# Message rows in three staggered steps, and a norm's chain moved among the projections

## The chip, the cores and the metric

The kernel runs on one core of a Trainium2 chip. The metric is the device time of one execution in microseconds (us), as the median of several runs. Every profile line below comes from one profiled execution.

The core has five engines with a queue each, and each works through its own queue in order: TensorE (PE in the profile, its weight loads PEld), VectorE (DVE), ScalarE (ACT), GpSimd (POOL) and SyncE (SP). DMAs are issued from the engines' queues, most of them here from SyncE's.

## What is computed

Four layers run one after another on an image batch of 4 x 128 x 128 x 128, each on the group-normalized output of the one before, with the result added to it: a deformable convolution, a scan of 1-d convolutions over rows, a message layer and a triangle layer. The change touches the last two. Cut to what matters:

```python
def _L2_conv_ref(inputs, Wself, Wm, Wk):
    message_m = jnp.sum(inputs, axis=2)
    message_k = jnp.sum(inputs, axis=1)
    z_self = jnp.einsum('bmkd,hd->bmkh', inputs, Wself)
    z_m = jnp.einsum('bmd,hd->bmh', message_m, Wm)[:, :, None, :]
    z_k = jnp.einsum('bkd,hd->bkh', message_k, Wk)[:, None, :, :]
    return z_self + z_m + z_k
...
    xn = layer_norm(x, norm_g, norm_b)
    left = xn @ left_w + left_b
    right = xn @ right_w + right_b
    left = left * jax.nn.sigmoid(xn @ lgate_w + lgate_b)
    right = right * jax.nn.sigmoid(xn @ rgate_w + rgate_b)
    out_gate = jax.nn.sigmoid(xn @ ogate_w + ogate_b)
    out = jnp.einsum('bkjd,bkid->bijd', left, right)
    out = layer_norm(out, onorm_g, onorm_b) * out_gate
    return out @ to_out_w + to_out_b
...
    x = x + _L2_conv_ref(_gn(x), L2_conv_Wself, L2_conv_Wm, L2_conv_Wk)
    x = x + _L3_conv_ref(_gn(x), L3_conv_norm_g, L3_conv_norm_b, L3_conv_left_w, L3_conv_left_b, L3_conv_right_w, L3_conv_right_b, L3_conv_lgate_w, L3_conv_lgate_b, L3_conv_rgate_w, L3_conv_rgate_b, L3_conv_ogate_w, L3_conv_ogate_b, L3_conv_onorm_g, L3_conv_onorm_b, L3_conv_to_out_w, L3_conv_to_out_b)
```

`_gn` normalizes groups of four channels over a whole image. So each layer needs the sums of all rows of an image before it can scale the first.

## The kernel before, in words

The first layer runs from the start to about 3340 us, the scan layer to about 4120 us, and the last two layers, in `message_and_triangle`, from there to the end at 5763 us. That function holds one whole image in SBUF (X, 128 channels by 128 by 128), the triangle's left factors and later its output (L), and two buffers R for a quarter of the channels of the right factors. R also takes quarters of the scan's output x2 from HBM, for the message rows of the next image.

For each image the work runs in these stages. All are lists of small Python functions, and `weave` deals pieces of several lists out in proportion to their lengths. The order of each engine's queue is the order in which the pieces are called: the scheduler is set to manual for all five engines (`manual_schedule`). A piece puts instructions into several queues at once, and those queues then run on their own.

1. **The norm of x2 (`prelude`, L1273).** A chain of small operations that goes to and fro between TensorE, VectorE and ScalarE: the group mean (L130 and L132), the variance (L134 to L140), square root and reciprocal (L86 to L90), the scaled weights ws, the sums msg and their products (L1277 to L1288), and the message vectors z with the channel sums (L1290 to L1302). It is one piece of the list.
2. **Message rows (`sums_of`, rows at L1315).** 32 blocks of four rows (JB = 4). A block is a product of ws with four rows of R into PSUM on TensorE (self_ps, L1319), four sums with the messages into X on VectorE (L1325), and one square with an accumulated sum on ScalarE (junk, L1330). All three stand in one piece. PSUM holds two such blocks (pool ps_q). After the block that empties a buffer R the next quarter of x2 is fetched into it. The pieces means, variances and close then give the scale for X.
3. **Turning (`turned`, L1401).** Four groups of 32 columns. A block of four columns is scaled (ScalarE, L1409), transposed on TensorE (turn_ps, L1419), copied back into X by ScalarE (L1420), and counted by bn_stats on VectorE (L1422). At the end of a group `factors` gives mean and reciprocal deviation.
4. **Spreading and projecting (`spread`, `projected`).** VectorE normalizes the turned columns (normed, L1439), TensorE transposes them back (back_ps, L1448), ScalarE copies (L1449). TensorE makes the gate and the left and right projections (proj_ps, L1479), eight columns to a piece, ScalarE their sigmoid (work, L1483), and VectorE two gated products into L and R (L1485). The first two quarters of the channels are projected among turning and spreading.
5. **Later projections and triangles (`projected`, `triangle`).** The third and fourth quarter, sixteen pieces each, are woven with eight pieces of the triangle product of the quarter before (tri_ps, L1497, copied to L by ScalarE, L1501). Then the last quarter's triangle runs alone.
6. **Output (`counted_out`, `given`).** VectorE counts columns of L (stats_o, L1512). A step of `given` loads a gate and x3 from HBM, normalizes four columns (two on VectorE, L1545, two on ScalarE, L1540), transposes them (gT_ps, L1555), scales them on ScalarE (work, L1557), multiplies by the gate on GpSimd (L1558), and in the step after that makes the output product (out_ps, L1565 and L1569), copied to res by ScalarE in odd steps (L1572) and by VectorE in even ones (L1574), and stored.

The next image's stages 1 and 2 and its first group of turning, together the list `ahead`, are woven into the output of the image before: the first six pieces (FIRST = 6) with the first group of counting, the others with the output steps. Image 0's run alone before, and nothing follows image 3's output. The columns of the last triangle are the first that the counting reads, so counting can't begin before the last copy into L.

Of the kernel before, what the change touches and what calls it, by code (L numbers as in the profile page):

```python
# [9 lines left out]
F32 = mybir.dt.float32  # L10
I32 = mybir.dt.int32
BF16 = mybir.dt.bfloat16
AF = mybir.ActivationFunctionType
# [5 lines left out]
P = 128  # L19
# [1155 lines left out]
def message_and_triangle(tc, c, x2T, x3d, gates, counted, w2, w3, out):  # L1175
# [15 lines left out]
    with ExitStack() as ctx:  # L1191
# [76 lines left out]
        def small_ps(shape, name):  # L1268
            return ps_g.tile(shape, F32, name=name, tag="ps_g")
# [2 lines left out]

        def prelude(b):  # L1273

            _, _, s2, t2 = gn_part(nc, c, two, two, ps_g, counted2[:, b], "x2", "ps_g")
            ws = one.tile([P, P], F32, name="ws")
            nc.vector.scalar_tensor_tensor(ws, wself, s2, c.ident, ALU.mult, ALU.add)  # L1277
            tsum = two.tile([P, 1], F32, name="tsum")
            nc.vector.tensor_scalar(tsum, t2, float(S), None, ALU.mult)
            msg = one.tile([P, 2, S], F32, name="msg")  # L1280
            nc.vector.tensor_scalar(msg[:, 0], sum_w[:, b], s2, tsum, ALU.mult, ALU.add)
            nc.vector.tensor_scalar(msg[:, 1], sum_h[:, b], s2, tsum, ALU.mult, ALU.add)
            twide = one.tile([P, S], F32, name="twide", tag="junk")
            nc.vector.tensor_scalar(twide, c.ones, t2, None, ALU.mult)
            pm = small_ps([P, 2, S], "msg_ps")
            nc.tensor.matmul(pm[:, 0], lhsT=wm, rhs=msg[:, 0], start=True, stop=False)
            nc.tensor.matmul(pm[:, 0], lhsT=wself, rhs=twide, start=False, stop=True)
            nc.tensor.matmul(pm[:, 1], lhsT=wk, rhs=msg[:, 1], start=True, stop=True)  # L1288
            z = one.tile([P, 2, S], F32, name="z")
            nc.vector.tensor_copy(z, pm)  # L1290
            zs = one.tile([P, 1], F32, name="zs")
            nc.vector.tensor_reduce(zs, z.rearrange("p a s -> p (a s)"), AX.X, ALU.add)
            sx = one.tile([P, 1], F32, name="sx")
            nc.vector.tensor_reduce(sx, sum_w[:, b], AX.X, ALU.add)
            pw = small_ps([P, 1], "sum_ps")
            nc.tensor.matmul(pw, lhsT=ws, rhs=sx, start=True, stop=True)
            less = two.tile([P, 1], F32, name="less3")
            nc.vector.scalar_tensor_tensor(less, zs, float(S), pw, ALU.mult, ALU.add)
            nc.vector.tensor_scalar(less, less, -1.0 / (S * S), None, ALU.mult)
            nc.vector.tensor_scalar(z[:, 1], z[:, 1], outb, None, ALU.add)  # L1300
            lessb = two.tile([P, 1], F32, name="lessb3")
            nc.vector.tensor_tensor(lessb, less, outb, ALU.subtract)  # L1302
            squares = two.tile([P, S // JB], F32, name="squares")
            got[b] = (ws, z, less, lessb, squares)

        def fetch(b, i):

# [2 lines left out]

        def sums_of(b):

            todo = [lambda: prelude(b)]

            def rows(y0):  # L1315
                ws, z, less, lessb, squares = got[b]
                at = y0 % DQ
                pz = ps_q.tile([P, JB, S], F32, name="self_ps", tag="ps_q")
                nc.tensor.matmul(  # L1319
                    pz, lhsT=ws, rhs=R[y0 // DQ % 2][:, at : at + JB, :], start=True, stop=True  # L1320
                )
                if at + JB == DQ and y0 + DQ < S:
                    fetch(b, y0 // DQ + 2)
                for i in range(JB):
                    nc.vector.scalar_tensor_tensor(  # L1325
                        X[:, :, y0 + i], pz[:, i], z[:, 0, y0 + i : y0 + i + 1], z[:, 1],
                        ALU.add, ALU.add,
                    )
                junk = one.tile([P, S, JB], F32, name="junk", tag="junk")
                nc.scalar.activation(  # L1330
                    junk, X[:, :, y0 : y0 + JB], AF.Square, bias=lessb,
                    accum_out=squares[:, y0 // JB : y0 // JB + 1],
                )

            todo += [lambda y0=y0: rows(y0) for y0 in range(0, S, JB)]
# [65 lines left out]
        def turned(b, g):  # L1401

            stats = two.tile([P, JG, 6], F32, name="stats_x")
            todo = []

            def scale(k):
                s3, t3 = got[b]
                js = slice(g * JG + k * JB, g * JG + (k + 1) * JB)
                nc.scalar.activation(X[:, js, :], X[:, js, :], AF.Identity, bias=t3, scale=s3)  # L1409

            def block(k):
                j0 = g * JG + k * JB
# [106 lines left out]
        def given(b):  # L1519
# [41 lines left out]
            def put(k):  # L1561
                xr, a = pend[k]
                po = ps_g.tile([P, JB, P], F32, name="out_ps", tag="ps_g")
                for j in range(JB):
                    nc.tensor.matmul(  # L1565
                        po[:, j], lhsT=xr[:, j], rhs=c.ident, is_transpose=True,
                        start=True, stop=False,
                    )
                    nc.tensor.matmul(po[:, j], lhsT=a[:, j], rhs=outw, start=False, stop=True)  # L1569
                res = three.tile([P, JB, P], F32, name="res")  # L1570
                if k % 2:
                    nc.scalar.copy(res, po)  # L1572
                else:
                    nc.vector.tensor_copy(res, po)  # L1574
                pend[k] = res
# [26 lines left out]
        def run(todo):  # L1602
            for f in todo:
                f()
# [99 lines left out]
```

## Time and profile before

| what | value |
|---|---|
| runs shown | 5764.49, 5773.65, 5774.59 us; median 5773.65 |
| the profiled execution | 5764.99 us, its span 5763.2 us |
| granted TensorE clock, mean | 0.956 |
| busy over the span | PE 5261.4 (91%), PEld 4488.0 (78%), DVE 3294.4 (57%), ACT 2781.5 (48%), POOL 779.5 (14%) |
| message rows of image 0, alone | 4138 to 4182 us |
| start of the projections, images 0 to 3 | 4220.9, 4629.3, 5035.7, 5442.0 us |
| message rows of images 1 to 3 (first to last sums) | 4439.0 to 4552.0, 4847.0 to 4958.2, 5253.3 to 5364.4 us |
| bn_stats of the turning waiting for ScalarE's copy (L1422) | 92.8 us in 88 waits |

How to read it: the busy time of an engine over the span is a mean of stages that differ, so the stages are looked at one by one. A line of waits reads "engine tile line <- who ended the wait: us in total, times, longest". In a list in order of time, a line is the start, the length, engine, line, operation, output <- input and shape, and in square brackets how long the engine had been idle and for whom.

### The profile page before, as it was taken

What the parts mean: (1) busy time and instruction counts of PE and PEld (TensorE: products, weight loads), DVE (VectorE), ACT (ScalarE), POOL (GpSimd) and SP (SyncE); (2) the same over time, 40 slices, a digit from 0 to 9 for tenths busy, and PEclk for the clock granted to TensorE, in tenths of its full rate; (3) what the DMA queues carried; (4) which work ended last, traced back from release to release, by engine and by line L of the source; (5) the groups of instructions that cost most, each with busy time, mean ns of one, the idle gap of its engine ahead of it and who ended that gap; (6) DMA issues with size and microseconds to landing.
All of it is one profiled execution on the core that took longest, in us unless ns stands there. A gap on an engine that the chain in (4) does not pass through costs nothing. (4 is left out here: it accounts for less than half of the span.)

```text
span 5763.2 us, 112068 instructions
## 1 busy us (share of the span) xinstructions
PE 5261.4 (91%) x42401; PEld 4488.0 (78%) x42401; DVE 3294.4 (57%) x10355; ACT 2781.5 (48%) x5852; POOL 779.5 (14%) x674
## 2 busy tenths in 40 slices
PE   2899999999999999999999979999788798798797
PEld 1778888888888888888888879999567577576686
DVE  5544444554444644444333279999865665656656
ACT  1355554455554555545544423333264664654755
POOL 2022111002110011111000012222100200201102
PEclk9899999999999999999999989999899899898899
DMA  4555555555554555555434222223221622513515
GB/s 145 135 138 131 136 129 120 127 124 136 128 134 107 129 129 134 131 125 124 93 75 80 54 86 89 89 90 98 96 115 58 209 88 94 199 59 128 192 41 167
DMA packets 1132346, 671.45 MB, mean 117 GB/s; under 512 B 736461, under 2 KB 1002894, under 8 KB 1113366
## 3 DMA queue, kind: packets, MB, share of 16 engines
q1 hardware_dynamic: 1121650, 657.77, 43.1%
q8 instruction: 338, 5.54, 0.4%
q10 hardware_dynamic: 10148, 6.43, 0.4%
q14 instruction: 210, 1.72, 0.1%
HBM read 382.88 MB, written 281.11 MB: 115 GB/s over the span
## 5 line engine op out<-in xcount | busy, mean ns | idle before, releaser
L509 DVE TENSOR_TENSOR m<-ty,t_ps 120x390 f32<-120x390 f32 x1548 | 804.5, 556 | 1503.6 <-ACT ty L507 1502.4
L520 PEld LDWEIGHTS v_ps<-m,pixels 120*128 120x128 f32 x11352 | 1439.2, 194 | 86.4 <-issue 10.1
L520 PE MATMUL v_ps<-m,pixels 120*128 120x108 f32 (+1 forms) x11352 | 1465.4, 273 | 3.6 <-ACT v L530 3.5
L530 ACT COPY v<-v_ps 128x432 f32<-128x432 f32 x1376 | 718.9, 522 | 1273.9 <-PE v_ps L520 1271.1
L578 PE MATMUL conv_ps<-v,wdef 128*128 128x128 f32 (+2 forms) x5160 | 1304.0, 379 | 5.0 <-DVE x1c L551 4.5
L578 PEld LDWEIGHTS conv_ps<-v,wdef 128*128 128x128 f32 x5160 | 814.2, 193 | 255.7 <-issue 24.9
L507 ACT COPY ty<-t_ps 120x390 f32<-120x390 f32 x1560 | 688.1, 489 | 179.4 <-PE t_ps L497 172.0
L497 PE MATMUL t_ps<-places,spread 25*120 25x99 bf16 (+1 forms) x10836 | 521.2, 260 | 63.2 <-DVE m L509 39.7
L497 PEld LDWEIGHTS <-spread 25*120 25x120 bf16 x10896 | 339.9, 137 | 225.4 <-issue 124.8
L1479 PEld LDWEIGHTS proj_ps<-wcat,X 128*128 128x128 f32 x4096 | 473.1, 192 | 29.6 <-issue 28.6
L1479 PE MATMUL proj_ps<-wcat,X 128*128 128x128 f32 x4096 | 480.6, 275 | 1.4
L392 POOL TENSOR_TENSOR off<-off,koff 72x512 f32<-72x512 f32 x128 | 162.1, 1267 | 2298.3 <-DVE off L389 2205.3
L1068 ACT ACTIVATE rowT<-x1T_ps,t_x,s_x 128x128 f32<-128x128 f32 x512 | 192.7, 457 | 366.4 <-PE x1T_ps L1061 346.8
L1558 POOL TENSOR_TENSOR work<-work,gate 128x512 f32<-128x512 f32 x128 | 163.3, 1276 | 1495.5 <-ACT work L1557 1245.4
L1081 PE MATMUL m_ps<-carry,w 128*128 128x172 f32 x2286 | 361.3, 310 | 0.0
L1485 DVE TENSOR_TENSOR L<-proj_ps,work 128x256 f32<-128x256 f32 x256 | 154.6, 604 | 340.5 <-ACT work L1483 340.5
L1081 PEld LDWEIGHTS m_ps<-carry,w 128*128 128x128 f32 x2286 | 345.5, 188 | 0.0
L1148 POOL TENSOR_TENSOR sum_h<-sum_h,x2c 128x512 f32<-128x512 f32 x128 | 162.3, 1268 | 1163.3 <-DVE x2c L1145 1163.3
L1483 ACT ACTIVATE work<-proj_ps 128x512 f32<-128x512 f32 x256 | 151.4, 597 | 283.9 <-PE proj_ps L1479 283.9
L1569 PE MATMUL out_ps<-outw,work 128*128 128x128 f32 x1024 | 219.0, 316 | 69.6 <-POOL work L1558 69.6
L1569 PEld LDWEIGHTS out_ps<-outw,work 128*128 128x128 f32 x1024 | 182.5, 223 | 86.8 <-POOL work L1558 86.8
L1325 DVE SCALAR_TENSOR_TENSOR X<-self_ps,z 128x128 f32<-128x128 f32 x512 | 152.4, 420 | 76.5 <-PE self_ps L1319 76.2
(230 smaller groups left out, 6675.5 us busy)
## 6 DMA issues: line engine op xcount, KB each, us to landing
pixels<-tab SPq DMA_DIRECT2D x688, 123.8 KB
xin<-in_x_dram SPq DMA_DIRECT2D x56, 1024.0 KB
off<-parts SPq DMA_DIRECT2D x64, 891.0 KB
tab<-rows SPq DMA_DIRECT2D x384, 128.0 KB
places<-off SPq DMA_DIRECT2D x688, 55.7 KB
x<-x1c SPq DMA_DIRECT2D x32, 1024.0 KB
x1rows<-x SPq DMA_DIRECT2D x128, 256.0 KB
x2T<-x2c SPq DMA_DIRECT2D x128, 256.0 KB
```

Source lines behind the costliest of these rows:

```text
L497: nc.tensor.matmul(to, lhsT=spread[p0 : p0 + KROWS, ph, :], rhs=mov, start=True, stop=True,)
L507: nc.scalar.copy(ty[:, 0:n], tp[0:LANES, 0, 0:n])
L509: nc.vector.tensor_tensor(m, ty[:, 0:n].rearrange("p (r c) -> p r c", c=PADW), tx, ALU.mult)
L520: nc.tensor.matmul(vp[:, h * n : h * n + rows * w].rearrange("p (k c) -> p k c", c=w), lhsT=pix[0:LANES, xb, :], rhs=m[:, :, RX * xb : RX ...
L530: nc.scalar.copy(v[:, :, c0 : c0 + 4 * RX].rearrange("p k (h c) -> p k h c", c=RX), vp[:, 0 : 4 * n].rearrange("p (h k c) -> p k h c", h=4 ...
L578: nc.tensor.matmul(pc[:, at : at + r1 - r0, :], lhsT=wdef[:, 3 * ky + kx, :], rhs=v[:, k0 + kx, r0:r1, kx : kx + S], start=m == 0, stop=m ...
L1068: nc.scalar.activation(rt[:, b, :], px[:, b, :], AF.Identity, bias=t, scale=s)
L1081: nc.tensor.matmul(to, lhsT=wgt, rhs=src[:, :, at : at + n], start=i == 0, stop=i + 1 == len(todo),)
L1148: nc.gpsimd.tensor_tensor(sum_h, sum_h, x2c[:, :, i], add)
L1479: nc.tensor.matmul(pp[:, j], lhsT=X[:, j0 + j, :], rhs=wcat[:, cols], start=True, stop=True)
L1558: nc.gpsimd.tensor_tensor(a, a, gt, ALU.mult)
L1569: nc.tensor.matmul(po[:, j], lhsT=a[:, j], rhs=outw, start=False, stop=True)
```

## The change

- **Rows in three steps.** `rows(k)` now issues the sums of block k-1, the product of block k and the squares of block k-2. There are 34 such pieces instead of 32.
- **The chain for the norm of x2 in six pieces.** `prelude` returns mean, variance, factors_of_x2, sums, messages and close. For images 1 to 3 they are woven into the projections of the last quarter of the image before; for image 0 they stand ahead of its rows, as before.
- **Counting of turned columns one block later.** bn_stats of block k-1 is issued after the copy of block k, and the last block's in the close.
- **Result copies.** VectorE copies every fourth result instead of every second.

With the six pieces of the chain, the sixteen of the projections and the eight of the triangle, `weave` gives this order (p projection, t triangle):

```
p0 t0 mean p1 p2 t1 p3 variance p4 t2 p5 p6 factors_of_x2 t3 p7 p8 t4 sums
p9 p10 t5 p11 messages p12 t6 p13 p14 close t7 p15
```

The diff, with the bodies of the chain's pieces left out where they are the old lines:

```diff
         def prelude(b):
 
-            _, _, s2, t2 = gn_part(nc, c, two, two, ps_g, counted2[:, b], "x2", "ps_g")
-            ws = one.tile([P, P], F32, name="ws")
...
+            v = {}
+
+            def mean():
+                v["ps"] = small_ps([P, 1], "gn_ps3")
+                nc.tensor.matmul(
+                    v["ps"], lhsT=c.gmean, rhs=counted2[:, b, 0:1], start=True, stop=True
+                )
+
+            def variance():
+                v["mean"] = two.tile([P, 1], F32, name="m_x2")
+                nc.vector.tensor_copy(v["mean"], v["ps"])
...
+                nc.tensor.matmul(v["ps"], lhsT=c.gmean, rhs=d, start=True, stop=True)
+
+            def factors_of_x2():
+                var = two.tile([P, 1], F32, name="gp_var")
+                nc.vector.tensor_copy(var, v["ps"])
+                _, v["s"], v["t"] = scale_shift(nc, c, two, v["mean"], var, "x2")
+
+            def sums():
+                s2, t2 = v["s"], v["t"]
...
+                nc.tensor.matmul(pm[:, 1], lhsT=wk, rhs=msg[:, 1], start=True, stop=True)
+
+            def messages():
+                z = v["z"] = one.tile([P, 2, S], F32, name="z")
+                nc.vector.tensor_copy(z, v["ps"])
...
+                nc.tensor.matmul(v["ps"], lhsT=v["ws"], rhs=sx, start=True, stop=True)
+
+            def close():
...
+                got[b] = (v["ws"], z, less, lessb, squares)
+
+            return [mean, variance, factors_of_x2, sums, messages, close]
 
         def sums_of(b):
 
-            todo = [lambda: prelude(b)]
...
+            def rows(k):
+                if 1 <= k <= n:
+                    put(k - 1)
+                if k < n:
+                    product(k)
+                if k >= 2:
+                    square(k - 2)
+
+            todo = [lambda k=k: rows(k) for k in range(n + 2)]
...
                 nc.scalar.copy(X[:, j0 : j0 + JB, :], pt)
-                for j in range(JB):
-                    nc.vector.bn_stats(stats[:, k * JB + j, :], X[:, j0 + j, :])
+                if k:
+                    count(k - 1)
+
+            def count(k):
+                for j in range(k * JB, (k + 1) * JB):
+                    nc.vector.bn_stats(stats[:, j, :], X[:, g * JG + j, :])
 
             def close():
+                count(JG // JB - 1)
                 known["x", b, g] = factors(stats, "x")
...
-                if k % 2:
+                if k % 4:
                     nc.scalar.copy(res, po)
                 else:
                     nc.vector.tensor_copy(res, po)
...
-        run(sums_of(0) + turned(0, 0))
+        run(prelude(0) + sums_of(0) + turned(0, 0))
...
             for q in range(2, NQ):
-                run(weave(projected(b, q, 0, S), triangle(b, q - 1)))
+                run(weave(
+                    projected(b, q, 0, S), triangle(b, q - 1),
+                    prelude(b + 1) if q + 1 == NQ and b + 1 < B else [],
+                ))
```

`product`, `put` and `square` hold the old lines of a row block's product with the fetch of R, its four sums and its square.

More of the change, by code (lines that the diff above doesn't have):

```diff
@@ L1273, in prelude @@
         def prelude(b):
-            _, _, s2, t2 = gn_part(nc, c, two, two, ps_g, counted2[:, b], "x2", "ps_g")
-            ws = one.tile([P, P], F32, name="ws")
[L1277 to L1304, printed above, removed]
+            v = {}
@@ new lines, in mean @@
+            def mean():
[6 more added lines that the diff above has]
+                nc.vector.tensor_copy(v["mean"], v["ps"])
+                d = two.tile([P, 1], F32, name="gp_d")
+                nc.vector.tensor_tensor(d, counted2[:, b, 0:1], v["mean"], ALU.subtract)
+                nc.vector.tensor_tensor(d, d, d, ALU.mult)
+                nc.vector.tensor_tensor(d, d, counted2[:, b, 1:2], ALU.add)
+                v["ps"] = small_ps([P, 1], "gn_ps4")
+                nc.tensor.matmul(v["ps"], lhsT=c.gmean, rhs=d, start=True, stop=True)
@@ new lines, in factors_of_x2 @@
+            def factors_of_x2():
[4 more added lines that the diff above has]
+                s2, t2 = v["s"], v["t"]
+                v["ws"] = one.tile([P, P], F32, name="ws")
+                nc.vector.scalar_tensor_tensor(v["ws"], wself, s2, c.ident, ALU.mult, ALU.add)
+                tsum = two.tile([P, 1], F32, name="tsum")
+                nc.vector.tensor_scalar(tsum, t2, float(S), None, ALU.mult)
+                msg = one.tile([P, 2, S], F32, name="msg")
+                nc.vector.tensor_scalar(msg[:, 0], sum_w[:, b], s2, tsum, ALU.mult, ALU.add)
+                nc.vector.tensor_scalar(msg[:, 1], sum_h[:, b], s2, tsum, ALU.mult, ALU.add)
+                twide = one.tile([P, S], F32, name="twide", tag="junk")
+                nc.vector.tensor_scalar(twide, c.ones, t2, None, ALU.mult)
+                pm = v["ps"] = small_ps([P, 2, S], "msg_ps")
+                nc.tensor.matmul(pm[:, 0], lhsT=wm, rhs=msg[:, 0], start=True, stop=False)
+                nc.tensor.matmul(pm[:, 0], lhsT=wself, rhs=twide, start=False, stop=True)
+                nc.tensor.matmul(pm[:, 1], lhsT=wk, rhs=msg[:, 1], start=True, stop=True)
@@ new lines, in messages @@
+            def messages():
+                z = v["z"] = one.tile([P, 2, S], F32, name="z")
+                nc.vector.tensor_copy(z, v["ps"])
+                v["zs"] = one.tile([P, 1], F32, name="zs")
+                nc.vector.tensor_reduce(v["zs"], z.rearrange("p a s -> p (a s)"), AX.X, ALU.add)
+                sx = one.tile([P, 1], F32, name="sx")
+                nc.vector.tensor_reduce(sx, sum_w[:, b], AX.X, ALU.add)
+                v["ps"] = small_ps([P, 1], "sum_ps")
+                nc.tensor.matmul(v["ps"], lhsT=v["ws"], rhs=sx, start=True, stop=True)
@@ new lines, in close @@
+            def close():
+                z = v["z"]
+                less = two.tile([P, 1], F32, name="less3")
+                nc.vector.scalar_tensor_tensor(
+                    less, v["zs"], float(S), v["ps"], ALU.mult, ALU.add
+                )
+                nc.vector.tensor_scalar(less, less, -1.0 / (S * S), None, ALU.mult)
+                nc.vector.tensor_scalar(z[:, 1], z[:, 1], outb, None, ALU.add)
+                lessb = two.tile([P, 1], F32, name="lessb3")
+                nc.vector.tensor_tensor(lessb, less, outb, ALU.subtract)
+                squares = two.tile([P, S // JB], F32, name="squares")
+                got[b] = (v["ws"], z, less, lessb, squares)
@@ L1311, in sums_of, with product @@
         def sums_of(b):
-            todo = [lambda: prelude(b)]
-            def rows(y0):
-                ws, z, less, lessb, squares = got[b]
+            n = S // JB
+            pending = {}
+            def product(k):
+                y0 = k * JB
+                ws = got[b][0]
+                pz = ps_q.tile([P, JB, S], F32, name="self_ps", tag="ps_q")
                 at = y0 % DQ
-                pz = ps_q.tile([P, JB, S], F32, name="self_ps", tag="ps_q")
                 nc.tensor.matmul(
@@ L1323, in rows, with put, square @@
                     fetch(b, y0 // DQ + 2)
+                pending[k] = pz
+            def put(k):
+                z, pz = got[b][1], pending.pop(k)
                 for i in range(JB):
+                    y = k * JB + i
                     nc.vector.scalar_tensor_tensor(
-                        X[:, :, y0 + i], pz[:, i], z[:, 0, y0 + i : y0 + i + 1], z[:, 1],
-                        ALU.add, ALU.add,
-                    )
-                junk = one.tile([P, S, JB], F32, name="junk", tag="junk")
+                        X[:, :, y], pz[:, i], z[:, 0, y : y + 1], z[:, 1], ALU.add, ALU.add,
+                    )
+            def square(k):
+                lessb, squares = got[b][3:]
+                junk = one.tile([P, S, JB], F32, name="junk")
                 nc.scalar.activation(
-                    junk, X[:, :, y0 : y0 + JB], AF.Square, bias=lessb,
-                    accum_out=squares[:, y0 // JB : y0 // JB + 1],
-                )
-            todo += [lambda y0=y0: rows(y0) for y0 in range(0, S, JB)]
+                    junk, X[:, :, k * JB : (k + 1) * JB], AF.Square, bias=lessb,
+                    accum_out=squares[:, k : k + 1],
+                )
+            def rows(k):
[6 more added lines that the diff above has]
+            todo = [lambda k=k: rows(k) for k in range(n + 2)]
             part = {}
```

## The prediction, made before the result was known

> **What bounds the kernel now.** I read the clock first (one core, 0.956), then the page's chain of work that ended last. That chain lies wholly in the last stage, so it says nothing of the others. So I cut the third part of the program (4138 to 5763 us) into stages by the starts of its tiles and asked for busy times in each (per row: stretch, length, busy us of each engine with its instructions, TensorE's granted clock, DMA share, GB/s):
>
> ```profile
> core 0: us, PE busy (x) PEld busy (x) DVE busy (x) ACT busy (x) POOL busy (x), PEclk, DMA share, GB/s
> 4340.00:4421.00 81.00, 79.60 (x707) 79.02 (x706) 34.57 (x67) 33.75 (x57) 0.00 (x0) 1.00 0.03 11
> 4437.00:4455.00 18.00, 12.12 (x15) 3.15 (x14) 17.27 (x69) 4.28 (x11) 0.00 (x0) 0.65 0.11 40
> 4455.00:4554.00 99.00, 73.74 (x346) 49.89 (x347) 74.38 (x249) 58.54 (x122) 22.86 (x18) 0.84 0.54 185
> 4629.00:4748.00 119.00, 107.26 (x721) 85.76 (x721) 72.59 (x241) 73.22 (x122) 0.00 (x0) 0.97 0.20 76
> ```
>
> The later projections with triangles (4340 to 4421) are bound by TensorE: busy 79.6 of 81, at full clock. The message rows among the output steps (4455 to 4554, image 1's rows in image 0's output) leave every engine idle for a quarter of the time or more. What VectorE and ScalarE wait for in that window:
>
> ```profile
> ACT junk L1330 <- DVE X L1325: 37.7, 23, 2.9
> DVE X L1325 <- PE self_ps L1319: 22.9, 10, 3.9
> ```
>
> VectorE's 74.4 busy and 22.9 waiting make 97.3 of 99: it is the engine of this stage, and the wait to remove is the one for a row block's product. Where it comes from shows in the order of time at one block:
>
> ```profile
> 4543.76 1.76 PE L1319 MATMUL self_ps<-R,ws 128*128 128x512 f32 x2
> 4545.56 1.23 DVE L1325 SCALAR_TENSOR_TENSOR X<-self_ps,z 128x128 f32<-128x128 f32 x4 [3.90 <-PE self_ps L1319]
> 4546.89 0.72 ACT L1330 ACTIVATE junk<-X,lessb 128x512 f32<-128x512 f32 x1 [2.30 <-DVE X L1325]
> ```
>
> The product stands on TensorE behind an output step (which itself waits for GpSimd: 13.1 us at L1569 here). VectorE's sums stand at the head of its queue until it lands, and ScalarE's squares until the sums land: three queues in one line. In the first stage of spreading and projecting (4629 to 4748) TensorE has 107.3 of 119 and its largest wait is
>
> ```profile
> PE back_ps L1448 <- DVE normed L1439: 7.3, 9, 2.5
> ```
>
> **The rows in three steps.** Sums of block k-1 now stand one list place behind their product, and squares one behind the sums. No instruction is added, the two PSUM buffers stay, the fetch of R stays glued to its product. Between product and sums there is now an output step's time or a block of statistics, so the 22.9 us should go. What is late next is VectorE itself: 74.4 busy, less 4.5 of 9 result copies in these 18 steps (k % 4 instead of k % 2) at 0.69 us = 3.1, leaves 71.3. ScalarE gets 58.5 + 4.5 x 0.58 + one square more (0.9) = 62; TensorE's 73.7 is at clock 0.84, at full clock some 55 to 62. The stage 4437 to 4455, without such waits, runs VectorE 17.27 of 18 (96%), which would give 74; ScalarE is close behind and the copy every fourth step still waits for TensorE in line (0.8 us once now), so I take 78.5: minus 20.5 an image, three images, **-61.5**. Ends: -26 (all waits and copies gone) and -10 (ScalarE and TensorE bring half of it back). Image 0's rows (4138 to 4182) run alone; VectorE has 36.3 of 44 and waits about 0.24 in every 2.49 us for the buffer's round trip, which is unchanged: 0. R's refill has eight blocks (about 22 us) against 7.4 from issue (4131.25) to first use (4138.65): hidden; without that cover, a wait of the difference.
>
> **The norm's chain taken from between the stages.** The last triangle ends on ScalarE at 4429.6; VectorE then does one block of statistics (1.1), and the next starts at 4437.60, after the chain. That is 6.9 us, three times: **-20.7**. Nothing else is late: R's first half is issued at 4417.87 and lands by about 4425.3 (7.4 later). Image 0's chain keeps its place: 0.
>
> **The same chain among the last projections.** The built order shows TensorE's matmuls of the chain directly behind the 4th, 9th and 12th of sixteen projection blocks (the middle one after a triangle block). TensorE is the bound there, and it waits for VectorE, where the chain stands behind that block's two products, which wait for ScalarE's sigmoid. The price of such a pass is in the trace, at the end of the stage:
>
> ```profile
> 4418.79 0.83 PE L1479 MATMUL proj_ps<-wcat,X 128*128 128x128 f32 x6
> ...
> 4419.71 0.60 ACT L1483 ACTIVATE work<-proj_ps 128x512 f32<-128x512 f32 x1 [1.25 <-PE proj_ps L1479]
> 4420.34 0.58 DVE L1485 TENSOR_TENSOR L<-proj_ps,work 128x256 f32<-128x256 f32 x1 [1.62 <-ACT work L1483]
> 4420.78 0.58 DVE L1485 TENSOR_TENSOR R<-proj_ps,work 128x256 f32<-128x256 f32 x1
> ...
> 4421.41 0.38 PE L1497 MATMUL tri_ps<-L,R 128*128 128x128 f32 x1 [1.79 <-DVE R L1485]
> ```
>
> So 1.75 us to R, then the chain's own VectorE time from its rows now. Variance: a copy and three columns, 4430.73 to 4431.45 = 0.75; wait 2.5, matmul 0.38: 2.9. Sums: ws, tsum, msg up to the matmul (4432.77 to 4433.62) 0.85, and the sigmoid ahead is late, because the factors switch ScalarE to the square root and back, and the first projection after it loses about 1.4 us. Counted from the end of the block before the switch: TensorE does a triangle block (to 0.9), two projections (2.7, 4.5) and a triangle (5.4); ScalarE has the root at 2.2, a copy at 2.8, the load at 4.1, its sigmoids at 4.7 and 5.3; VectorE the two blocks' products at 5.85 and 6.95, then 0.85: 7.8. The wait is 7.8 - 5.4 = 2.4; three matmuls and twide add 1.1: 3.5. Messages: z, zs and sx, 4435.33 to 4436.45 = 1.1; wait 2.85, matmul 0.38: 3.2. Mean: 0.28. Sum 9.9 an image, **+29.7**. Who pays behind the waiting matmul: every projection and triangle after it. VectorE's own 4 to 5 us of the chain lie in its idle 46 of 81; the chain issues no DMA, so SyncE's and GpSimd's queues are not touched. Ends: +2.2 an image (matmuls only, if the waits fell into slack) and +15.
>
> Two rules of the Trainium skill speak against this placing. "ScalarE: Activation LUTs", What ACT_TABLE_LOAD costs, prices a switch of function set at a load of 1283 ns and a drain of some 1380, 2.66 us. The row here is a load of 1.28 at 4629.64, with the activation starting at 4630.94 directly behind it. By the row the delay is the 1.4 above; by the page the middle wait grows by 1.4, +4.2 in all. I keep the row. "TensorE: Matmul & The Clock Gate", What's actually happening, has TensorE fall to half clock after an idle window of about 3.4 us. In the trace the 1.79 us gap above left the clock at 1.00 (4419 to 4424), while the 6.55 us one before 4138.65 was followed by products at half pace. My gaps of 2.5 to 2.9 are nearer the first: no loss; by the page's window a gap that joined a second one could lose about 3.4/2 = 1.7 each, which is in the +15.
>
> **Statistics one block later in the turning.** VectorE's bn_stats waited for ScalarE's copy (92.8 us over the run, L1422) with the norm that TensorE waits for behind it. Moved behind the next block's copy, it finds its data ready. The close does the last block, as before. Of the 7.3 (7.7 in image 0) I count 5 in each of four images, since ScalarE's copy into the same two buffers (TensorE waits 2.1 for it) comes next: **-20**. Ends: 0 and -8.
>
> **The rest.** In the last image VectorE is the fullest engine (88.7 of 113, ScalarE 67.3); eight copies less are 5.5 us of VectorE, 4.7 more of ScalarE, of which **-3** may show; the 46 us parts with turning (ScalarE 33) I put at 0. Ends: +6 and -6.
>
> Sum: -61.5 - 20.7 + 29.7 - 20 - 3 = **-75.5**. The profiled execution took 5764.99 (span 5763.2), so 5689.5 by its own time. It lies at the lower end of the runs (5764.49, 5773.65, 5774.59); a median after could lie by either, so I add half of the 8.7 between: **5694**.
>
> **Rivals.** (1) ScalarE and TensorE take over in the rows: half of the gain turns into new waits of the copies for out_ps; 99 becomes 88. -33 instead of -61.5: 5722. For it: three engines between 62 and 74 of 99. Against: the last image runs with the same three-way coupling and VectorE there goes from operation to operation. (2) The chain costs its matmuls alone, because TensorE catches up after each wait in slack that the busy time hides: +6.6 instead of +29.7: 5671. Against it: TensorE's 79.6 of 81. (3) Slower: the chain's waits on TensorE cost the upper 15 an image, and the rows only rename their wait, because the output step's own loop through GpSimd (13.1 us of TensorE's waits) sets their pace. Then -20.7 + 45 - 5 - 3 = +16: 5786. This side begins where rows and statistics together save less than the 9 us by which the chain costs more than it frees (29.7 - 20.7). Against it: GpSimd is busy 22.9 of 99.
>
> **How the numbers follow.** Mine 0.58 (5670 to 5718), rival 1 0.20, rival 2 0.13, rival 3 0.05, and 0.04 for no visible change, where the gain is eaten by the chain. The range for 8 in 10 takes mine, rival 2 and most of rival 1: 5648 to 5740. About 0.2% (11 us) is what a measurement of this kernel tells from no change. Faster 0.90, same 0.05, slower 0.05.
>
> **What would show it.** Rows: VectorE's wait for self_ps in the output stage near 0 and the stage near 78 us; TensorE's wait for "normed" in the turning falls under 3; new rows "gn_ps", "msg_ps", "sum_ps" waiting for VectorE at 2.4 to 2.9 us each, three to an image; the last projections' stage longer by 10; the first message rows right behind the last triangle. I am wrong if the rows' stage stays above 90, or if the chain's waits are absent.

## The result, and the profile after

| | before | after |
|---|---|---|
| median of the runs, us | 5771.17 (5764.49 to 5774.59, 4 runs) | 5690.13 (5682.31 to 5692.68, 4 runs) |
| ratio, 95% interval | | 0.9869 [0.9849, 0.9889] |
| profiled execution, its span, us | 5764.99, 5763.2 | 5688.34, 5686.6 |
| granted TensorE clock, mean | 0.956 | 0.964 |

The change makes the kernel 1.3% faster. The forecast was 5694, by a sum of -75.5 us on the profiled execution; that execution became 76.7 us shorter. But the sum came out right partly because errors cancelled, and that shows only stage by stage. The table cuts the last two layers of both profiled executions by the starts of the same instructions. It counts from the first sums of image 0's rows, since what lies ahead of them is the work of the layers before and differs by up to 20 us from one profiled execution to the next (the first sums start between 4125.1 and 4144.6 in the versions below).

| stage, us for images 0, 1, 2 (and 3) | before | after | change in all | predicted |
|---|---|---|---|---|
| image 0's rows and turning, alone | 80.2 | 77.4 | -2.8 | 0 |
| projections with turning (to the first triangle) | 119.4, 119.1, 118.9, 120.2 | 118.3, 116.8, 116.7, 118.5 | -7.3 | -20 |
| later projections and triangles (to the first output count) | 89.3, 89.3, 89.3, 89.3 | 100.3, 103.4, 100.3, 89.3 | +36.1 | +29.7 |
| first count to first sums, and the rows | 122.4, 120.5, 120.5 | 92.8, 96.6, 92.7 | -81.3 | -82.2 |
| last sums to the next projection (turning among output) | 77.3, 77.5, 77.6 | 69.9, 71.8, 70.3 | -20.4 | 0 |
| image 3's output | 111.7 | 109.9 | -1.8 | -3 |
| sum | 1622.5 | 1545.0 | -77.5 | -75.5 |

The stages in the profile after, image 0 (columns as in the windows before: stretch, length, busy us and instructions by engine, granted clock, DMA share, GB/s). The four rows are the later projections, the rows, the turning and the next image's first projections:

```profile
core 0: us, PE busy (x) PEld busy (x) DVE busy (x) ACT busy (x) POOL busy (x), PEclk, DMA share, GB/s
4337.30:4437.60 100.30, 91.48 (x782) 89.92 (x783) 37.71 (x86) 41.07 (x68) 0.00 (x0) 0.98 0.06 22
4452.00:4530.40 78.40, 62.70 (x333) 42.52 (x333) 73.77 (x249) 59.84 (x127) 22.80 (x18) 0.92 0.66 228
4530.40:4600.30 69.90, 53.22 (x347) 42.97 (x348) 46.10 (x174) 58.46 (x105) 18.20 (x15) 0.93 0.72 267
4600.30:4717.10 116.80, 105.83 (x723) 84.79 (x721) 71.89 (x243) 72.03 (x122) 0.00 (x0) 0.99 0.20 77
```

The rows' row answers to the 99-us one before: as many VectorE instructions (249, with four sums more and four result copies fewer) are busy 73.77 us, before 74.38, but in 78.4 us. The wait for self_ps, 22.9 before, is in VectorE's list no more:

```profile
DVE res L1629 <- PE out_ps L1624: 2.6, 2, 1.7
DVE r_o L1442 <- ACT r_o L1441: 0.9, 3, 0.3
```

With 0.9 more for its result copies, all its waits come to 4.4 us. VectorE goes straight from sums to statistics to the next sums, and now TensorE is the one that stands: 13.4 us of self_ps for VectorE's X, at no cost, because VectorE (94% busy) sets the end.

TensorE's waits in image 1's later projections are now the chain's three, beside the 1.8 that was there before:

```profile
PE sum_ps L1322 <- DVE sx L1320: 2.7, 1, 2.7
PE gn_ps L1291 <- DVE gp_d L1289: 2.4, 1, 2.4
PE msg_ps L1310 <- DVE msg L1305: 1.9, 1, 1.9
PE tri_ps L1552 <- DVE R L1540: 1.8, 1, 1.8
```

The three come to 7.0 us; 7.75 were predicted (2.4 for msg_ps, 2.5 for gn_ps, 2.85 for sum_ps). One of them in the order of time, in image 0, with the sixteen projections ahead of it:

```profile
4388.06 1.95 PE L1534 MATMUL proj_ps<-wcat,X 128*128 128x128 f32 x16
...
4391.17 0.57 DVE L1540 TENSOR_TENSOR R<-proj_ps,work 128x256 f32<-128x256 f32 x1
4391.60 0.15 DVE L1285 COPY m_x<-gn_ps 128x1 f32<-128x1 f32 x1
...
4392.19 0.16 DVE L1289 TENSOR_TENSOR gp_d<-gp_d,counted 128x1 f32<-128x1 f32 x1
...
4392.40 0.38 PE L1291 MATMUL gn_ps<-gp_d,gmean 128*128 128x1 f32 x2 [2.39 <-DVE gp_d L1289]
...
4392.65 3.27 PE L1534 MATMUL proj_ps<-wcat,X 128*128 128x128 f32 x16
```

VectorE needs 0.75 us for the variance, but stands behind the two gated products, which stand behind the sigmoid. Behind the wait there is a cost that the prediction put at nothing: the sixteen projections after it take 3.27 us, where the sixteen before it took 1.95. TensorE runs at about half clock for a while. In image 1 this follows all three waits, at once or up to 2 us later; two such stretches of image 1 (the columns are those of the windows above; the number before the DMA share is the clock):

```profile
4771.90:4775.20 3.30, 2.97 (x14) 2.97 (x15) 0.24 (x2) 0.00 (x0) 0.00 (x0) 0.53 0.00 0
4789.30:4793.00 3.70, 3.70 (x22) 3.70 (x21) 0.19 (x1) 0.60 (x1) 0.00 (x0) 0.56 0.00 0
```

### The profile page after: what moved, and what is told of

The parts are those of the page before. It is cut to its first block, busy times and chain, and to the rows that moved or that the text cites. A ratio compares the mean times of both kernels' runs of the same rounds, so it can differ in the third digit from the quotient of the medians.

```text
span 5686.6 us, 112077 instructions
## 1 busy us (share of the span) xinstructions
PE 5214.1 (92%) x42401; PEld 4461.0 (78%) x42401; DVE 3277.2 (58%) x10323; ACT 2798.5 (49%) x5890; POOL 780.3 (14%) x674
## 5 line engine op out<-in xcount | busy, mean ns | idle before, releaser
L1624 PE MATMUL out_ps<-outw,work 128*128 128x128 f32 x1024 | 193.8, 292 | 34.1 <-POOL work L1613 33.5
L1354 PE MATMUL self_ps<-R,ws 128*128 128x512 f32 x256 | 157.6, 705 | 70.1 <-DVE X L1365 60.9
L1624 PEld LDWEIGHTS out_ps<-outw,work 128*128 128x128 f32 x1024 | 164.8, 203 | 46.8 <-POOL work L1613 46.8
## 6 DMA issues: line engine op xcount, KB each, us to landing
places<-off SPq DMA_DIRECT2D x688, 55.7 KB
```

## The experiments

The theory at this point: (a) the rows' steps gain their 60 us by themselves; (b) the chain among the projections costs waits of TensorE and the half clock behind them, which exceeds what its old place cost; (c) the later statistics act mostly in the turning. The rivals: that the parts need each other, and that the chain's move pays by letting the rows begin earlier. Ratios are to the kernel before, run beside each version on the same chip.

### One part at a time

**Rows alone**: the kernel before with the three-step rows (`rows(k)` as in the change), and nothing else. Of the edit, the list:

```diff
-            todo = [lambda: prelude(b)]
+            todo = [lambda: prelude(b)] + [lambda k=k: rows(k) for k in range(n + 2)]
```

> The kernel before with only the rows staggered; the chain stays one piece ahead of the rows. Theory (the wait of VectorE's sums for their product was the whole loss of the rows' stage): the stage from the first output count to the last sums goes from 122 to about 100 us an image, VectorE's wait for self_ps in it from 22.9 to under 2, in all about -60 us (ratio 0.9895). Rival (the stage moved with the chain and the fewer copies as well, and the rows gave only part): -30 us or less, with waits of 8 us or more left on VectorE.

Measured: 5697.13 us, 0.9881 [0.9865, 0.9898]. The rows took 95.0, 93.6 and 92.3 us (before 113.0, 111.2, 111.1), and the turning 71.2, 68.8, 70.8 (before 77.3 to 77.6). Counted from image 0's first sums the execution was 77.0 shorter: as much as the whole change. The rows with the gap ahead of them gave 48.8 of it, the turning 21.6, the projections 7.1. VectorE's wait for self_ps is gone from its list here too, so the steps alone remove it. But 60 us were expected, all from the rows, and 28.7 came elsewhere. Image 0's projections and the turning after image 1's rows, first before, then with the rows alone:

```profile
4220.90:4340.30 119.40, 107.24 (x722) 85.65 (x720) 72.56 (x239) 72.89 (x122) 0.00 (x0) 0.97 0.19 76
4552.00:4629.30 77.30, 58.09 (x339) 45.98 (x338) 45.65 (x177) 57.31 (x101) 17.77 (x14) 0.87 0.66 238
4220.70:4337.50 116.80, 104.56 (x723) 83.96 (x721) 72.63 (x239) 72.75 (x122) 0.00 (x0) 1.00 0.20 77
4533.00:4604.20 71.20, 51.71 (x335) 40.87 (x336) 47.27 (x177) 55.61 (x98) 17.23 (x14) 0.95 0.70 259
```

In both stages TensorE was busy for less time at a higher clock, while it waited as long as before (11.4 us for 11.3 in the projections, 19.5 for 19.1 in the turning). Why the clock was higher there was not tried.

**The chain alone**: the kernel before with the chain in six pieces among the last projections. Of the edit, the call:

```diff
-                run(weave(projected(b, q, 0, S), triangle(b, q - 1)))
+                run(weave(
+                    projected(b, q, 0, S), triangle(b, q - 1),
+                    prelude(b + 1) if q + 1 == NQ and b + 1 < B else [],
+                ))
```

> The kernel before with only the chain for x2's norm in six pieces among the last projections. Theory (three waits of TensorE in line, 2.4, 1.9 and 2.7 us, its matmuls, and half clock behind some of the waits): the stage with the last projections grows by 11 to 14 us an image, the gap ahead of the rows shrinks by 6.9, in all about +15 us, slower (ratio 1.0026). Rival (the chain pays for itself, its place costs what it frees): within 3 us of before.

Measured: 5773.63 us, 1.0007 [0.9998, 1.0016]. The later stage grew to 104.9, 98.6 and 100.3 us, the gap before the first sums shrank from 9.4 to 1.1. That is 2.7 us by the medians, where 15 were expected, with 1 inside the interval: by itself the move brings nothing, and the rival of this run (within 3 us) fits. Its profiled execution is 6.6 longer from image 0's first sums on: 35.9 more in the later stage, 24.7 less in the gaps, 6.7 less in the turnings, and 2.1 more in the other stages.

Image 1 shows what the three waits cost without the half clock. TensorE waits 2.4, 1.9 and 2.7 us as in the change, and the clock stays at 1.00:

```profile
4752.20:4850.80 98.60, 89.78 (x782) 88.29 (x783) 37.58 (x85) 41.05 (x68) 0.00 (x0) 1.00 0.06 22
```

That is 9.3 over the 89.3 without a chain.

**Statistics alone**: bn_stats of a block of turned columns issued one block later (the close counts the last block).

```diff
-                for j in range(JB):
-                    nc.vector.bn_stats(stats[:, k * JB + j, :], X[:, j0 + j, :])
+                if k:
+                    count(k - 1)
```

> The kernel before with only the statistics of the turning one block later. Theory (a part of the 20 us by which the turning among the output and the first turning became shorter in the changed kernel is due to it, besides the 7 us in the projections): -15 to -25 us, TensorE's wait for normed in the first projections under 3 us. Rival (only the projections' 7 us are due to it, the turning among the output became shorter because its clock and its transfers changed with the rows): -7 us, the stretch from the last sums to the next projections stays at 77 us.

Measured: 5745.57 us, 0.9957 [0.9940, 0.9973]. The turning lost 4.4, 5.5 and 5.1 us; the projections only 1.0, 0.8, 3.1 and 1.5, and image 0's rows and turning 2.7. The rows of images 2 and 3 took 5 us longer (116.4 and 116.1), for a reason that these runs do not show, so from the first count to the next projection only 4.8 us of the turning's 15.0 are left: (c) holds by the cut at the last sums, not for the whole stretch. The wait for normed is 4.2, not under 3 as expected. By its stages the profiled execution is 13.9 shorter, by the medians 25.4; the expected 15 to 25 lie between.

**Copies alone**: `k % 4` for `k % 2`.

```diff
-                if k % 2:
+                if k % 4:
```

> The kernel before with only the result copies changed (VectorE every fourth instead of every second). Theory (VectorE waits in the rows' stage anyway, and is the fullest engine only in the last image's output): -2 to -5 us, nearly all in the last image's output. Rival (ScalarE, which has the added copies in line with the squares, becomes late): 0 to +5 us.

Measured: 5753.95 us, 0.9986 [0.9977, 0.9995]. The turnings are shorter by 2.6 to 2.8 us each and image 3's output by 2.3. So it is 6.6 us by the medians where 2 to 5 were expected, and mostly in the turnings, where the output of the last image was expected.

**Everything but the chain**: the kernel after, with the chain in one piece ahead of the rows again.

```diff
-            todo = [lambda k=k: rows(k) for k in range(n + 2)]
+            todo = [lambda: [f() for f in prelude(b)]] + [lambda k=k: rows(k) for k in range(n + 2)]
...
-                run(weave(
-                    projected(b, q, 0, S), triangle(b, q - 1),
-                    prelude(b + 1) if q + 1 == NQ and b + 1 < B else [],
-                ))
+                run(weave(projected(b, q, 0, S), triangle(b, q - 1)))
```

> The changed kernel with the chain put back as one piece ahead of the rows; rows, statistics and copies as changed. Theory (the chain among the projections costs more than it frees): faster than the changed kernel by about 15 us, near 5675 (ratio to before 0.9835). Rival (behind the staggered rows the chain ahead of them would cost more than 6.9 us, since their product waits for it too): no faster than the changed kernel, 5690 or more.

Measured: 5663.31 us, 0.9811 [0.9794, 0.9827]. This is faster than the change itself, with intervals apart. From image 0's first sums it is 102.0 shorter than before; rows, statistics and copies alone gave 77.0, 13.9 and 10.3, together 101.2, so in total these three parts add up. Stage by stage they don't: from the first count to the next projection they gave 81.5 alone and 90.1 together, in the projections 15.2 alone and 6.9 together. So the rival that the parts need each other falls for the total alone. Against the change the later stage is shorter by 36.1 and the turning by 6.9, while the gap with the rows is longer by 18.6 (the first sums come 11.3 after the first count instead of 2.2, 27.2 in three images, but the rows are 8.7 shorter). So the move frees 18.6, of which 6.9 is given back in the turning, and costs 36.1: a net loss of 24.5 in the changed kernel, small differences in the other stages included. (b) holds, and the rival that the move pays by an earlier start falls.

### Is it the wait, or the matmuls and their place?

**Products one piece behind their data**: the chain stays among the projections, but each of its three waiting TensorE products is a piece of its own, dealt out after the next projection or triangle.

```diff
                 nc.vector.tensor_tensor(d, d, counted2[:, b, 1:2], ALU.add)
+                v["d"] = d
+
+            def variance_product():
                 v["ps"] = small_ps([P, 1], "gn_ps4")
...
-            return [mean, variance, factors_of_x2, sums, messages, close]
+            return [
+                mean, variance, variance_product, factors_of_x2, sums, sums_product,
+                messages, messages_product, close,
+            ]
```

> The changed kernel with each TensorE product of the chain one piece behind the VectorE piece that feeds it (nine pieces instead of six); the same instructions, both switches of ScalarE's function set kept. Theory (the chain's cost is TensorE's waits in line and the half clock that follows them): no wait of gn_ps, msg_ps or sum_ps over 0.8 us, the granted clock of that stage 1.00, the stage 92 to 94 us instead of 100 to 103, in all about -25 us against the changed kernel, near 5664. Rival (the cost is the function switches and VectorE's added work): the stage stays at 98 us or more.

Measured: 5658.01 us, 0.9817 [0.9801, 0.9834]. The later stage takes 92.0, 91.9, 91.9 us at a clock of 1.00. TensorE's waits in image 0's stage, then the stage's window (columns as above):

```profile
PE tri_ps L1565 <- DVE R L1553: 1.8, 1, 1.8
PE proj_ps L1547 <- DVE R L1553: 0.9, 1, 0.9
```

```profile
4321.00:4413.00 92.00, 89.23 (x783) 88.18 (x783) 37.75 (x86) 41.09 (x68) 0.00 (x0) 1.00 0.06 24
```

The same products in the same stage now cost 2.7 us over the 89.3 without a chain, instead of 11 to 14. No line of the chain is in the list; 0.9 is the wait after the change of ScalarE's function set. What was lost was the wait, and one piece of distance removes it. Over the whole the version is no faster than the one that leaves the chain ahead of the rows (0.9817 and 0.9811, the intervals almost the same; 1521.4 and 1520.5 us from image 0's first sums): what it frees in one stage it loses in others. The way back, from the square root to the sigmoid, reads in the order of time:

```profile
4380.26 0.29 ACT L86 ACTIVATE std_x<-gp_var,eps 128x1 f32<-128x1 f32 x1
4380.57 1.28 ACT L1551 ACT_TABLE_LOAD   x1
...
4381.86 0.60 ACT L1551 ACTIVATE work<-proj_ps 128x512 f32<-128x512 f32 x1
```

The sigmoid starts directly behind the load, as the square root did behind its own (4378.96 for 1.28, then 4380.26). The load's row of 1.28 is the whole cost on ScalarE, and the drain of "ScalarE: Activation LUTs", What ACT_TABLE_LOAD costs, which the prediction had set aside, is not seen.

**Filling the gaps**: the change, with nine spare 128x128 products issued into TensorE's queue ahead of each waiting product (81 more for images 1 to 3).

```diff
+                for _ in range(FILL if b else 0):
+                    nc.tensor.matmul(
+                        t[:, 384:512], lhsT=c.ident, rhs=c.ident, start=True, stop=True
+                    )
```

> The changed kernel with nine spare 128x128 products on TensorE (about 2 us, of no use for the output, which stays the same) ahead of each of the chain's three waiting products for images 1 to 3, so that TensorE has work while it waits. Theory (the waits are followed by half clock because TensorE stood idle): granted clock 1.00 in the stage, the projection blocks behind the waits at 1.95 us instead of 3.3, the stage 98 to 100 us in all three images instead of 100.3, 103.4, 100.3, in all 3 to 7 us faster than the changed kernel although 81 products were added. Rival (the slow blocks have another cause): the slow blocks stay, and the kernel is the same or slower.

Measured: 5676.39 us, 0.9854 [0.9837, 0.9870]. The stage of images 0 and 1, in the same columns:

```profile
4330.60:4429.40 98.80, 95.86 (x836) 94.32 (x837) 37.76 (x86) 41.11 (x68) 0.00 (x0) 1.00 0.06 22
4713.00:4811.80 98.80, 95.83 (x838) 94.34 (x837) 37.87 (x86) 40.95 (x68) 0.00 (x0) 1.00 0.06 22
```

The clock stays at 1.00, and all three images take the same 98.8 us, where the change took 100.3, 103.4 and 100.3: 7.6 less with more work. The half clock is thus a cost of the gaps, of 1.5 us in images 0 and 2, where the clock fell once, and 4.6 in image 1, where it fell three times; the other 9.5 are waits and products, the spare ones included. The image of the chain alone in which the clock did not fall agrees, with 98.6 and no spare products. It also shows that such a gap need not be followed by half clock; of the six images with these gaps one escaped it, and of the three with the gaps filled all did. Over whole runs the two intervals overlap, so this reading rests on the stage, not on the median.

**Less of the chain**: mean, variance and factors made once for all four images ahead of image 0; per image only sums, messages and their products remain, each product one piece behind its data.

```diff
-            return [mean, variance, factors_of_x2, sums, messages, close]
+            return [sums, sums_product, messages, messages_product, close]
...
-        run(prelude(0) + sums_of(0) + turned(0, 0))
+        run([factors_of_all] + prelude(0) + sums_of(0) + turned(0, 0))
```

> The changed kernel with mean, variance and factors of x2's norm made once for all four images ahead of image 0's rows (one chain, four columns wide), and only sums, messages and close of each image among the last projections, their products one piece later. Theory: the stage with the last projections 90 to 92 us (89.3 without a chain), no switch of ScalarE's function set in it, in all about -30 us against the changed kernel, near 5660, the fastest of all. Rival (the products' place still costs several us): the stage over 95 us.

Measured: 5657.97 us, 0.9808 [0.9791, 0.9824]. The later stage is 90.2 in all three images, 0.9 over none. The gain over the split version is not seen in the median: its rows took 95.9, 94.8 and 90.0 us, at a TensorE clock of 0.86, 0.86 and 0.91.

### Why the earlier rows pay so little

In the split version the first sums come 9.1 us sooner after the first count than with the chain ahead of the rows, and still the stretch from that count to the next projection is only 3.8 shorter (mean of three: 164.8 against 168.6). Both profiles show TensorE waiting for x3's columns in the turning, at a DMA share of about 0.7. So transfers could hold it. To test this, both kernels were run without the load of the gate in the output steps. The multiplication stays, but by ones, which leaves that gate's part of the computation out; the tile through which the projections write the gate has two buffers instead of three.

```diff
-                gt = three.tile([P, JB, S], F32, name="gate", tag="load")
-                nc.sync.dma_start(gt, gates[b, :, k * JB : (k + 1) * JB, :])
-                pend[k] = (gt,)
+                pend[k] = (ungated,)
```

> This is the version with the chain in nine pieces among the last projections, but the output steps load no gate: the normalized output is multiplied by ones (this part of the computation is left out, so its time stands only beside that of its partner without gates, which has the chain in one piece ahead of the rows). With gates, the stretch from an image's first output count to the next image's first projection took 164.8 us here and 168.7 in the partner: 3.9 less, though 5.6 us of VectorE's chain lie elsewhere. Theory A (transfers hold the turning, so what an earlier start of the rows frees is given back while TensorE waits for x3's columns): with a third of the loads gone that wait falls under 1 us in both, the turning stage gets shorter by 3 us or more in this kernel (70 to 67 or less), and the stretch here becomes at least 6 us shorter than the partner's. Theory B (the turning is held by ScalarE and the output step that falls into it): the turning stays within 2 us of 70, and the difference of the stretches stays at about 4.

> The partner: the chain in one piece ahead of the rows, and again no gate is loaded in the output steps (multiplied by ones: that part of the computation is left out). With gates its stretch from first output count to next projection took 168.7 us, its turning 69.0, 67.4 and 68.7. Theory A (transfers): the turning falls by less here than in the split version, by 0 to 2 us, because the rows start later against the same transfers; the stretch is at least 6 us longer than the split version's. Theory B (ScalarE and the output step): turning within 2 us of 68, stretch about 4 longer than the split version's.

Measured, one execution each: 5653.06 (split) and 5658.05 (one piece), beside 5771.92 for the kernel before. The turning took 69.1, 69.7, 69.6 in the split version and 67.0, 67.5, 65.4 in the other; the stretches were 163.7 and 165.6, a difference of 1.9. TensorE's waits in a window over the turning in image 0's output, 4530 to 4605 us, first the split version with gates, then without:

```profile
PE turn_ps L1482 <- ACT X L1472: 2.6, 2, 2.3
PE out_ps L1633 <- DMA x3cols<-x3d: 2.4, 1, 2.4
PE turn_ps L1482 <- ACT X L1483: 2.3, 7, 1.1
```

```profile
PE turn_ps L1484 <- ACT X L1485: 4.7, 8, 2.0
PE turn_ps L1484 <- ACT X L1474: 3.2, 3, 2.3
PE gT_ps L1623 <- ACT work L1625: 2.3, 3, 1.1
```

The wait for the transfer is gone, and the turnings are only 0.9 shorter in the mean (1.7 in the other version). The waits for ScalarE and GpSimd took its place: turn_ps from 4.9 to 7.9, gT_ps from 0.9 to 2.3, and out_ps for GpSimd from 4.9 to 6.0. Theory A, which had 3 us or more here, falls: the turning is bound mainly by other things than the transfers. Theory B named ScalarE and the output step; the turning fits it (within 2 us of 70, and of 68 but for one image), the difference of the stretches (1.9, not 4) doesn't. Which of the two takes the freed time back stays open.

## Why the prediction was right, and where it wasn't

- **The rows: right in mechanism and in size.** The step "the 22.9 us should go, and VectorE is late next" shows as the missing wait, which the rows alone remove as well, and VectorE's 73.77 of 78.4 us, where 78.5 was predicted. With the gap, -81.3 against -82.2. The first rival (ScalarE and TensorE take over, 88 us) falls in the same row: ScalarE is busy 59.84, and its copies wait 6.1 for out_ps.
- **The chain taken from between the stages: right in the stage, too much in the whole.** The gap fell by 7.1 to 7.2 us where 6.9 was predicted. But "nothing else is late" was wrong: the version without the move shows 6.9 of the 18.6 given back in the turning.
- **The chain among the projections: the mechanism right, the size +36.1 for +29.7.** The three waits were 7.0 us for 7.7, and without half clock an image's chain cost 9.3 (image 1 of the chain alone) where the sum had 9.9. The step that failed is "gaps of 2.5 to 2.9 are nearer the 1.79 gap: no loss". The clock fell to about half after five of the nine waits. The prediction had this cost, 1.7 a gap, in its upper end; filling the gaps measured 1.5 in two images and 4.6 in the third, about 1.5 a fall. The window of about 3.4 us of "TensorE: Matmul & The Clock Gate", What's actually happening, would have spoken for no loss too; these rows decide against it for these gaps. The second rival, that the chain costs its matmuls alone, falls for this placing, and is nearly true (2.7) for the one with one piece of distance.
- **Statistics: too much put on the projections.** -5 an image was put on the projections, because "it finds its data ready". TensorE's waits there, image 1:

```profile
PE back_ps L1503 <- DVE normed L1494: 4.2, 3, 2.6
PE turn_ps L1469 <- ACT X L1459: 2.2, 2, 1.9
PE turn_ps L1469 <- ACT X L1470: 2.1, 2, 1.1
PE back_ps L1503 <- ACT gate L1513: 1.2, 4, 0.3
```

The wait for normed fell from 7.3 to 4.2, not under 3: six short waits are gone and the three at the starts of groups remain, behind `factors`, which the close still makes wait for the last block. 1.2 came back as a wait for the gate's copy and 0.7 for turn_ps. In the four images TensorE's waits fell from 44.0 to 38.4, so of the 7.3 that the projections gained at most 5.6 are waits, not 20. The rest is TensorE's busy time, which varies with its clock: the rows alone gained 7.1 here with all nine waits for normed still there.
- **The turning among the output: a term put at nothing that was 20.4.** "The 46 us parts with turning I put at 0" failed. VectorE's wait of statistics in the turning after image 1's rows, before and after:

```profile
DVE stats_x L1422 <- ACT X L1420: 20.3, 14, 3.8
DVE stats_x L1476 <- ACT X L1470: 7.8, 8, 4.3
```

But this wait does not set the length of the stage. With the statistics alone it falls to 3.6 and the turning by 4.4 us; with the rows alone it stays at 15.4 and the turning falls by 6.1. What goes with the length is TensorE's busy time: in the three turnings 174.3 before, 158.9 after and 155.2 with the rows alone, at a clock of 0.87, 0.93 and 0.95, while its waits are 57.8, 55.7 and 55.7. So most of the 20.4 is TensorE's busy time, 15.4 less at a higher clock, which the forecast did not count on; why the clock rose stays open. Rows, statistics and copies alone shorten these turnings by 21.6, 15.0 and 8.2, and all three by 27.3: they do not add up there. By the cut at the last sums, part of the rows' gain may also fall into this stage.
- **The total.** Statistics and projections gained 12.7 less than put down and the chain cost 6.4 more; the turning, and image 0's 2.8 (the statistics alone gave 2.7 there), gave 23.2 more. That the forecast lies within 4 us of the median is owed to this balance, which is luck. The third rival (slower) needed rows and statistics to save less than 9 us; the rows alone saved 77.

## What to carry to other kernels

Where several engines pass a block along, issue each engine's step one block behind the one that feeds it: by itself that took the time to 0.9881 here, of the whole change's 0.9869, with no operation and no buffer added. A chain of small operations that is dealt into a busy engine's queue needs the same distance: glued to its feeder each product held TensorE for 2 to 3 us, and an image's chain cost 11 to 14 us in the change; with one piece of distance it cost 2.7, and the tested versions with that distance, or with the chain outside that queue, took 0.981 of the time before against 0.987. None of them is measurably faster than the one that leaves the chain where it was, so no gain of the move itself is shown here. Forecast each stage by itself and check it by itself, since a right total can hold errors of 6 to 20 us that cancel.

## What the runs showed of the hardware

- **Half clock after short gaps.** In the changed kernel TensorE's clock fell to 0.53 to 0.61 for 3 to 4 us after gaps of 2.39 us in three of three cases, and after gaps of 1.92 and 2.69 us in one of three each; gaps of 1.79 us at the end of the same stage left it at 1.00 in all three images (4430 to 4437, 4812 to 4821, 5197 to 5206 us). With the chain alone it fell after the same gaps in two, none and one of three, twice for 6 us (0.50 and 0.51 at 4394.1 to 4400.3 and 4421.8 to 4428.0). So the length of the gap alone does not decide, and what does was not found. With spare products in the gaps the clock was 1.00 in all three images.
- **The clock outside these gaps.** With the rows alone it rose from 0.87 to 0.95 in the turning, with TensorE's waits as they were. As the rows' waits went, TensorE's clock there rose from 0.84 to 0.92, and within one execution of the version with factors made once it was 0.86 in two images and 0.91 in the third, whose rows were 5 us shorter. Which is cause and which effect was not tried.
